# Stacking the parts of q and k of an attention layer by transfers through DRAM instead of products with selection matrices

## The chip, the cores and the metric

The kernel runs on one core of one Trainium2 chip. The metric is device time of one execution in microseconds (us). All compared runs were in the fast state, unless the text says otherwise. In the profiles PE is TensorE, PEld its weight loads, DVE VectorE, ACT ScalarE, POOL GpSimd and SP SyncE. The granted clock is the share of TensorE's full clock that the throttle allowed, as the profiler recorded it. A transfer lands when its completion is signalled.

## The reference

Four graph layers on 4096 nodes with 128 features, each followed by a residual and a layer norm. Only layer 1 matters here, a masked attention with four heads of 32 columns:

```python
N, IN, H, C = (4096, 128, 4, 32)
q = (x @ Wq + bq).reshape(n, H, C)
k = (x @ Wk + bk).reshape(n, H, C)
v = (x @ Wv + bv).reshape(n, H, C)
attn = jnp.einsum('nhc,mhc->hnm', q, k) / np.float32(np.sqrt(C))
mask = adj == 0.0
# ... softmax over the unmasked m gives alpha; out = alpha @ v per head ...
x_r = x @ Ws + bs                      # the "residual rows"
beta = jax.nn.sigmoid(jnp.concatenate([out, x_r, out - x_r], axis=-1) @ Wb)
return beta * x_r + (1.0 - beta) * out
```

## The kernel before

The scores are products in a rounded float32 format (float32r). To keep accuracy, k and q are cut into a rounded part `hi` and a rest `lo`. A head has only 32 of the 128 contraction rows, so the four combinations hi·hi, hi·lo, lo·hi and lo·lo are put below one another: for each head, rows 0..127 of `KS` hold hi, hi, lo, lo of k, and those of `QS` hold hi, lo, hi, lo of q. One product then gives the full score. The kernel before makes these stacks on PE, with selection matrices:

```python
def stacked(psum, a, hi, lo, h2):                     # two heads per call: four products
    p = psum.tile([P, 2, S], F32, tag="s", name="pst")
    for h in range(2):
        nc.tensor.matmul(p[:, h, :], lhsT=sel[a][:, 0, h2 + h, :], rhs=hi, start=True, stop=False)
        nc.tensor.matmul(p[:, h, :], lhsT=sel[a][:, 1, h2 + h, :], rhs=lo, start=False, stop=True)
    return p
```

The product stage, once per chunk c of 512 nodes (eight chunks):

```python
nc.tensor.matmul(p, lhsT=wk, rhs=XT[:, s], start=True, stop=True)
nc.scalar.activation(hi, p, AF.Identity, bias=bkc)
nc.vector.scalar_tensor_tensor(lo, p, bkc, hi.bitcast(F32), op0=ALU.add, op1=ALU.subtract)
nc.vector.tensor_reduce(mx[:, 1, c : c + 1], hi.bitcast(F32), AX.X, ALU.max, ...)
nc.scalar.copy(KS[:, 0:2, s], stacked(ps_s, 1, hi, lo, 0))
nc.vector.tensor_copy(KS[:, 2:4, s], stacked(ps_s, 1, hi, lo, 2))
# ... q likewise, written whole to DRAM (qd); only chunk 0 is cut and stacked here ...
```

Then come the V additions, and the residual rows in eight groups, each through one of two buffers to DRAM:

```python
r = rot.tile([P, 4, D], F32, tag="r", name="r")       # rot: bufs=2
nc.vector.tensor_tensor(r, p, bsr.unsqueeze(1).to_broadcast([P, 4, D]), ALU.add)
nc.sync.dma_start(out=rd[:, g[0] : g[-1] + 1, :], in_=r)
```

Attention follows: eight blocks of 512 queries, 32 steps of 128 keys each, where a step has four score products, two exponentials (ACT), a mask (DVE) and eight products for the weighted sums. Its working buffers take the memory of the product stage's. During block I the queries of block I+1 are fetched, cut and stacked:

```python
if I + 1 < NS:
    if jb == 5:
        fetch_queries(I + 1)                          # 256 KB from DRAM
    if jb == 18:
        cut_queries()                                 # ACT copy, DVE subtraction
    if jb in (21, 25):
        stack_queries(I + 1, (jb - 21) // 2)          # four products, one ACT cast
```

## Time and profile before

| | us |
|---|---|
| time, median of 3 runs | 2435.04 (2432.41 to 2437.69) |
| profiled span | 2427.1 |
| layer 0 ends (last group-norm activation starts) | 950.55 |
| first weighted sum of attention | 1043.21 |
| first weighted sum of attention's last step | 1868.4 |

The first layer runs the same code in all kernels here, and yet its end lies between 949.0 and 955.0 us in the profiles of this study. So I compare the second layer from that landmark on. Its two parts are called **entry** (from layer 0's end to the first weighted sum: 92.7 us in the kernel before) and **loop** (from there to the first weighted sum of the last step: 825.2 us).

The prediction quotes the windows, the chain and the timeline. One line more will be needed, the writes of the residual rows in the timeline of SP (start, length of the group of issues, engine, line, what, count):

```profile
1021.18 10.87 SPq L877 DMA_DIRECT2D rd<-r  x8
```

The reader is to see that eight writes took 10.87 us to issue; each had to wait for its row addition, and that for one of the two buffers.

### The profile page before, as it was taken

To read this page: it belongs to the slowest core of one execution; us is meant where nothing else is said; L and a number is where in the kernel's file an instruction comes from. 1 tells how busy PE (TensorE), PEld (TensorE's weight loads), DVE (VectorE), ACT (ScalarE), POOL (GpSimd) and SP (SyncE) were. 2 spreads that over 40 slices of the span, in tenths; PEclk is the share of its full clock that TensorE was granted. 3 is DMA by queue.
4 is the path that set the end of the run, shared out by engine and by line. 5 is a ranking of instruction groups with operands and counts; after the bars stand their busy time and mean duration, and the time that the engine had idled before them with its cause. 6 is when DMAs were issued, how large, how long until landed. Compare 5 with 4: busy or idle time off the path is not lost.

```text
span 2427.1 us, 24381 instructions
## 1 busy us (share of the span) xinstructions
PE 2048.1 (84%) x8923; PEld 1138.3 (47%) x8923; DVE 1910.2 (79%) x2726; ACT 1486.0 (61%) x1793; POOL 69.5 (3%) x87
## 2 busy tenths in 40 slices
PE   4477887787777771889999999999998899979998
PEld 4266666566666650634333333433333344444443
DVE  6478888788778888767877878777787887668887
ACT  5688889888888877478777787878776000010000
POOL 2000000000000051100000000000000000000000
PEclk7689989899888885999999999999999899979999
DMA  2455466555555630154454444545444788528774
GB/s 52 139 185 200 143 207 210 172 181 183 186 169 173 195 105 1 61 200 171 154 182 153 168 173 154 176 158 179 158 160 162 279 287 284 206 104 298 286 286 170
DMA packets 103768, 431.44 MB, mean 178 GB/s; under 512 B 8976, under 2 KB 19280, under 8 KB 62672
## 3 DMA queue, kind: packets, MB, share of 16 engines
q1 hardware_dynamic: 85200, 295.50, 35.9%
q10 hardware_dynamic: 18432, 134.23, 15.9%
q8 instruction: 74, 1.21, 0.2%
q14 instruction: 62, 0.51, 0.1%
HBM read 356.26 MB, written 73.43 MB: 177 GB/s over the span
## 4 chain that ended last, share of the span: by engine, by line
PE 58%; DVE 24%; ACT 12%; issue 3%; DMA 2%; SPq 0%; ACTq 0%; POOL 0%; DVEq 0%; POOLq 0%
PE pv L965 15%; PE pa L1357 9%; PE pa L1212 9%; PE ps L939 9%; DVE e L948 5%; PE pz L583 4%; DVE w L606 3%; PE pi L674 3%; DVE w L636 3%; DVE t L632 3%; PE ptA L564 3%; ACT t L628 3%; ACT e L946 2%; ACT at L572 2%; ACT w L601 1%
## 5 line engine op out<-in xcount | busy, mean ns | idle before, releaser
L948 DVE SCALAR_TENSOR_TENSOR e<-at,e 128x2048 f32<-128x2048 f32 x256 | 581.6, 2287 | 181.0 <-ACT e L946 171.3
L946 ACT ACTIVATE e<-ps 128x1024 f32<-128x1024 f32 x512 | 489.4, 1025 | 130.6 <-PE ps L939 101.8
L965 PE MATMUL pv<-e,VA 128*64 128x512 f32 x2048 | 503.5, 613 | 12.2 <-DVE e L948 12.2
L939 PE MATMUL ps<-QS,KS 128*128 128x512 f32 x1024 | 313.1, 425 | 27.7 <-ACT e L946 23.3
L939 PEld LDWEIGHTS ps<-QS,KS 128*128 128x128 f32 x1024 | 173.3, 190 | 246.0 <-ACT e L946 153.6
L674 PE MATMUL pi<-HA,w 128*128 128x129 f32 x1152 | 186.7, 337 | 83.2 <-DVE w L636 83.2
L965 PEld LDWEIGHTS pv<-e,VA 128*64 128x64 f32 x2048 | 126.0, 137 | 258.1 <-issue 232.2
L1357 PE MATMUL pa<-w,F 128*128 128x512 f32 x512 | 223.2, 597 | 12.2 <-DVE w L1354 12.2
L674 PEld LDWEIGHTS pi<-HA,w 128*128 128x128 f32 x1152 | 179.8, 249 | 93.8 <-DVE w L636 93.8
L1212 PE MATMUL pa<-at,Y 128*128 128x512 f32 x512 | 223.1, 596 | 0.0
L1354 DVE SCALAR_TENSOR_TENSOR w<-rho,col,at 128x512 f32<-128x512 f32 x256 | 186.7, 746 | 18.9 <-PE pa L1357 1.7
L591 DVE SCALAR_TENSOR_TENSOR t<-ei,de,pz 128x512 f32<-128x512 f32 x144 | 107.2, 747 | 106.5 <-PE pz L583 102.7
L564 PE MATMUL ptA<-ident,ad 128*128 128x128 f32 x1032 | 146.0, 287 | 42.9 <-ACT at L572 35.7
L1222 DVE SCALAR_TENSOR_TENSOR odd<-at 128x2048 f32<-128x2048 f32 x64 | 146.6, 2290 | 38.3 <-DMA at<-adjT 37.6
L564 PEld LDWEIGHTS ptA<-ident,ad 128*128 128x128 f32 x1032 | 124.9, 148 | 99.4 <-ACT at L572 53.3
L572 ACT COPY at<-ptA 128x512 f32<-128x512 f32 x200 | 108.3, 587 | 99.0 <-PE ptA L564 98.8
L583 PE MATMUL pz<-HT 128*128 128x512 f32 x292 | 161.6, 664 | 4.9 <-DVE w L655 4.5
L1357 PEld LDWEIGHTS pa<-w,F 128*128 128x128 f32 x512 | 97.3, 192 | 133.9 <-issue 100.1
L1212 PEld LDWEIGHTS pa<-at,Y 128*128 128x128 f32 x512 | 97.5, 192 | 120.0 <-issue 118.8
L606 DVE TENSOR_TENSOR w<-w,at 128x2048 f32<-128x2048 f32 x64 | 143.7, 2281 | 0.0
L1361 ACT COPY a<-pa 128x512 f32<-128x512 f32 x8 | 4.7, 586 | 206.1 <-PE pa L1357 206.1
L931 ACT ACTIVATE nat<-nat 128x2048 f32<-128x2048 f32 x64 | 122.7, 1918 | 1.9 <-DMA nat<-in_adj_dram 1.9
(351 smaller groups left out, 2448.8 us busy)
## 6 DMA issues: line engine op xcount, KB each, us to landing
at<-adjT SPq DMA_DIRECT2D x128, 1024.0 KB, 4.8
ad<-in_adj_dram SPq DMA_DIRECT2D x64, 1024.0 KB, 6.5
adjT<-at SPq DMA_DIRECT2D x64, 1024.0 KB, 8.3
nat<-in_adj_dram ACTq DMA_DIRECT2D x64, 1024.0 KB, 4.9
at<-adjT ACTq DMA_DIRECT2D x64, 1024.0 KB, 4.8
dj<-rows SPq DMA_DIRECT2D x28, 256.0 KB, 7.6
X<-in_x_dram SPq DMA_DIRECT2D x4, 512.0 KB, 6.5
di<-rows SPq DMA_DIRECT2D x8, 256.0 KB, 8.4
```

The source lines that it names most:

```text
L564: nc.tensor.transpose(pt[:, ib, :], st[p]["ad"][k][:, ib, jb * P : (jb + 1) * P], self.ident)
L572: copy(st[p]["at"][k][:, jb, :], st[p]["pt"].pop(m))
L583: nc.tensor.matmul(pz, lhsT=HT[:, j * P : (j + 1) * P], rhs=HT[:, I * S : (I + 1) * S], start=True, stop=True)
L606: nc.vector.tensor_tensor(w, w, at, ALU.mult)
L674: nc.tensor.matmul(self.po[ib // 2][:, ib % 2, :], lhsT=w[0][:, jb, ib * P : (ib + 1) * P], rhs=HA[:, 4 * J + jb, :], start=False, stop=(J ...
L939: nc.tensor.matmul(p[:, h, :], lhsT=KS[:, h2 + h, jb * P : (jb + 1) * P], rhs=QS[I % 2][:, h2 + h, :], start=True, stop=True,)
L946: nc.scalar.activation(e[:, h2 : h2 + 2, :], p, AF.Exp)
L948: nc.vector.scalar_tensor_tensor(e, at[:, jb % 4, :].unsqueeze(1).to_broadcast([P, NH, S]), 0.0, e, op0=ALU.not_equal, op1=ALU.mult,)
L965: nc.tensor.matmul(st["po"][h // 2][g : g + 64, :], lhsT=VA[:, o : o + 64], rhs=e[:, h, :], start=(jb == 0), stop=(jb == NT - 1), skip_gro ...
L1212: nc.tensor.matmul(pa, lhsT=Y[:, 4 * J + jb, :], rhs=at[:, jb, :], start=False, stop=(J == NS - 1 and jb == 3), skip_group_check=True,)
L1354: nc.vector.scalar_tensor_tensor(w, rho[:, I * S : (I + 1) * S], col[:, 0, j : j + 1], at[:, jb, :], op0=ALU.max, op1=ALU.mult)
L1357: nc.tensor.matmul(pa, lhsT=F[:, j, :], rhs=w, start=False, stop=(j == NT - 1), skip_group_check=True)
```

## The change

The intent is to free PE of the selection products, since PE bounds both the product stage and the loop. All chunks of k and q are cut once, both parts go to DRAM in one write of 512 KB, and a stack is made by four reads of 256 KB, each to 32 partitions. The destination is float32r, and GpSimd issues the reads; the prediction says why.

```diff
-            sel = [keep.tile([P, 2, NH, P], F32R, ...) for k in range(2)]
-            qd = self.dram.tile([P, N], F32, tag="qd", name="qd")
+            qk = self.dram.tile([2, 2, P, N], F32, tag="qk", name="qk")
-            def stacked(psum, a, hi, lo, h2): ...
+            def stack(a, dst, c):
+                for r, part in enumerate(((0, 1, 0, 1), (0, 0, 1, 1))[a]):
+                    nc.gpsimd.dma_start(
+                        out=dst[r * C : (r + 1) * C, :, :],
+                        in_=qk[a, part, :, c * S : (c + 1) * S].rearrange("(h c) n -> c h n", h=NH),
+                    )
@@ product stage, per chunk c
+                    for a, w, bias in ((1, wk, bkc), (0, wq, bqc)):
+                        p = self.ps_t.tile([P, S], F32, tag="pt", name="pqk")
+                        nc.tensor.matmul(p, lhsT=w, rhs=XT[:, s], start=True, stop=True)
+                        cut = rot.tile([P, 2, S], F32R, tag="cut", name="cut", bufs=4)
+                        nc.scalar.activation(cut[:, 0, :], p, AF.Identity, bias=bias)
+                        nc.vector.scalar_tensor_tensor(cut[:, 1, :], p, bias, cut[:, 0, :].bitcast(F32), ...)
+                        nc.vector.tensor_reduce(mx[:, a, c : c + 1], cut[:, 0, :].bitcast(F32), ...)
+                        nc.sync.dma_start(out=qk[a, :, :, s].rearrange("k p n -> p k n"), in_=cut.bitcast(F32))
+                        if a:
+                            stack(1, KS[:, :, s], c)
+                        elif c < 2:
+                            stack(0, QS[c], c)
@@ attention loop
-                        if I + 1 < NS: ...            # fetch, cut, stack at steps 5, 18, 21, 25
+                        if jb == 3 and 0 < I < NS - 1:
+                            stack(0, QS[(I + 1) % 2], I + 1)
```

The branch for large scores (not taken with these inputs) is adapted too; it is left out here. So are two small edits: `Wq` is scaled by 1/sqrt(C) beforehand, and the PSUM pool of these products has eight buffers instead of four, in place of the pool of the selection products.

More of the change, by code (lines that the diff above doesn't have):

```diff
@@ L781, in layer1 @@
             QS = [keep.tile([P, NH, S], F32R, tag=f"QS{k}", name=f"QS{k}") for k in range(2)]
-            sel = [keep.tile([P, 2, NH, P], F32R, tag=f"sel{k}", name=f"sel{k}") for k in range(2)]
-            qd = self.dram.tile([P, N], F32, tag="qd", name="qd")
+            qk = self.dram.tile([2, 2, P, N], F32, tag="qk", name="qk")
             rd = self.dram.tile([P, NT, D], F32, tag="rd", name="rd")
@@ L793, in layer1 @@
             bvr, bsr = self.load_row(bv, "bvr"), self.load_row(bs, "bsr")
-            for a, rows in enumerate((((0, 2), (1, 3)), ((0, 1), (2, 3)))):
-                nc.gpsimd.memset(sel[a].bitcast(F32), 0.0)
-                for b in range(2):
-                    for r in rows[b]:
-                        nc.gpsimd.tensor_copy(
-                            sel[a][:, b, :, r * C : (r + 1) * C], self.ident.rearrange("p (h c) -> p h c", h=NH)
-                        )
-            def stacked(psum, a, hi, lo, h2):
-                p = psum.tile([P, 2, S], F32, tag="s", name="pst")
-                for h in range(2):
-                    nc.tensor.matmul(p[:, h, :], lhsT=sel[a][:, 0, h2 + h, :], rhs=hi, start=True, stop=False)
-                    nc.tensor.matmul(p[:, h, :], lhsT=sel[a][:, 1, h2 + h, :], rhs=lo, start=False, stop=True)
-                return p
+            def stack(a, dst, c):
[4 more added lines that the diff above has]
+                    )
             with ExitStack() as pctx:
@@ L813, in layer1 @@
                 rot = pctx.enter_context(tc.tile_pool(name="rot1", bufs=2))
-                self.ps_t = pctx.enter_context(tc.tile_pool(name="ps_t", bufs=4, space=PSUM))
-                ps_s = pctx.enter_context(tc.tile_pool(name="ps_s1", bufs=2, space=PSUM))
+                self.ps_t = pctx.enter_context(tc.tile_pool(name="ps_t", bufs=8, space=PSUM))
                 nc.gpsimd.memset(VA, 1.0)
@@ L821, in layer1 @@
                 nc.vector.tensor_scalar(bqc, bqc, 1.0 / math.sqrt(C), None, op0=ALU.mult)
+                nc.vector.tensor_scalar(wq, wq, 1.0 / math.sqrt(C), None, op0=ALU.mult)
                 for c in range(NC):
                     s = slice(c * S, (c + 1) * S)
-                    p = self.ps_t.tile([P, S], F32, tag="pt", name="pk")
-                    nc.tensor.matmul(p, lhsT=wk, rhs=XT[:, s], start=True, stop=True)
-                    hi = rot.tile([P, S], F32R, tag="hi", name="hi")
-                    lo = rot.tile([P, S], F32R, tag="lo", name="lo")
@@ L828, in layer1 @@
-                    nc.scalar.activation(hi, p, AF.Identity, bias=bkc)
-                    nc.vector.scalar_tensor_tensor(lo, p, bkc, hi.bitcast(F32), op0=ALU.add, op1=ALU.subtract)
-                    nc.vector.tensor_reduce(
-                        mx[:, 1, c : c + 1], hi.bitcast(F32), AX.X, ALU.max, apply_absolute_value=True
-                    )
-                    nc.scalar.copy(KS[:, 0:2, s], stacked(ps_s, 1, hi, lo, 0))
-                    nc.vector.tensor_copy(KS[:, 2:4, s], stacked(ps_s, 1, hi, lo, 2))
@@ L835, in layer1 @@
-                    p = self.ps_t.tile([P, S], F32, tag="pt", name="pq")
-                    nc.tensor.matmul(p, lhsT=wq, rhs=XT[:, s], start=True, stop=True)
-                    q = rot.tile([P, S], F32, tag="q", name="q")
-                    nc.scalar.activation(q, p, AF.Identity, bias=bqc, scale=1.0 / math.sqrt(C))
-                    nc.sync.dma_start(out=qd[:, s], in_=q)
-                    nc.vector.tensor_reduce(mx[:, 0, c : c + 1], q, AX.X, ALU.max, apply_absolute_value=True)
-                    if c == 0:
-                        hi = rot.tile([P, S], F32R, tag="hi", name="hi")
-                        lo = rot.tile([P, S], F32R, tag="lo", name="lo")
-                        nc.scalar.copy(hi, q)
-                        nc.vector.tensor_tensor(lo, q, hi.bitcast(F32), ALU.subtract)
-                        for h2 in range(0, NH, 2):
-                            nc.scalar.copy(QS[0][:, h2 : h2 + 2, :], stacked(ps_s, 0, hi, lo, h2))
+                    for a, w, bias in ((1, wk, bkc), (0, wq, bqc)):
[3 more added lines that the diff above has]
+                        nc.scalar.activation(cut[:, 0, :], p, AF.Identity, bias=bias)
+                        nc.vector.scalar_tensor_tensor(
+                            cut[:, 1, :], p, bias, cut[:, 0, :].bitcast(F32), op0=ALU.add, op1=ALU.subtract
+                        )
+                        nc.vector.tensor_reduce(
+                            mx[:, a, c : c + 1], cut[:, 0, :].bitcast(F32), AX.X, ALU.max, apply_absolute_value=True
+                        )
+                        nc.sync.dma_start(out=qk[a, :, :, s].rearrange("k p n -> p k n"), in_=cut.bitcast(F32))
[3 more added lines that the diff above has]
+                            stack(0, QS[c], c)
@@ L880, in layer1, with attention_unshifted @@
             with tc.If(small > 0) as cmp:
-                self.attention_unshifted(VA, KS, QS, stacked, qd, rd, wb)
+                self.attention_unshifted(VA, KS, QS, stack, rd, wb)
             with cmp.Else():
-                self.attention_shifted(V, qd, (wk, bkc), rd, wb)
-    def attention_unshifted(self, VA, KS, QS, stacked, qd, rd, wb):
+                self.attention_shifted(V, qk, rd, wb)
+    def attention_unshifted(self, VA, KS, QS, stack, rd, wb):
         nc, tc, N, NT, NS, D, X = self.nc, self.tc, self.N, self.NT, self.NS, self.D, self.X
@@ L896, in attention_unshifted @@
             st = {}
-            def fetch_queries(I):
-                st["f"] = rot.tile([P, S], F32, tag="f", name="f")
-                nc.sync.dma_start(out=st["f"], in_=qd[:, I * S : (I + 1) * S])
-            def cut_queries():
-                hi = rot.tile([P, S], F32R, tag="hi", name="hi")
-                lo = rot.tile([P, S], F32R, tag="lo", name="lo")
-                nc.scalar.copy(hi, st["f"])
-                nc.vector.tensor_tensor(lo, st["f"], hi.bitcast(F32), ALU.subtract)
-                st["parts"] = hi, lo
-            def stack_queries(I, h2):
-                nc.scalar.copy(QS[I % 2][:, h2 : h2 + 2, :], stacked(ps_s, 0, *st["parts"], h2))
             def load(I, J):
@@ L1048, in attention_unshifted @@
                             degree(8 * I + jb // 4)
-                        if I + 1 < NS:
-                            if jb == 5:
-                                fetch_queries(I + 1)
-                            if jb == 18:
-                                cut_queries()
-                            if jb in (21, 25):
-                                stack_queries(I + 1, (jb - 21) // 2)
+                        if jb == 3 and 0 < I < NS - 1:
+                            stack(0, QS[(I + 1) % 2], I + 1)
                         scores(I, jb)
@@ L1068, in attention_unshifted, with attention_shifted @@
             nc.vector.tensor_tensor(self.deg, self.deg2[:, 0, :], self.deg2[:, 1, :], ALU.add)
-    def attention_shifted(self, V, qd, kw, rd, wb):
+    def attention_shifted(self, V, qk, rd, wb):
         nc, tc, N, NT, D, X = self.nc, self.tc, self.N, self.NT, self.D, self.X
@@ L1079, in attention_shifted @@
             KT = keep.tile([P, N], F32, tag="KT", name="KT")
-            XT = keep.tile([P, S], F32, tag="XT", name="XT")
-            for g in self.groups():
-                s = slice(g[0] * P, (g[-1] + 1) * P)
-                p = self.ps_t.tile([P, 4, P], F32, tag="pt", name="pt")
-                for k, t in enumerate(g):
-                    nc.tensor.transpose(p[:, k, :], X[:, t, :], self.ident)
-                nc.vector.tensor_copy(XT, p.rearrange("p a b -> p (a b)"))
-                p = self.ps_t.tile([P, 4, P], F32, tag="pt", name="pt").rearrange("p a b -> p (a b)")
-                nc.tensor.matmul(p, lhsT=kw[0], rhs=XT, start=True, stop=True)
-                nc.scalar.activation(KT[:, s], p, AF.Identity, bias=kw[1])
+            K2 = keep.tile([P, S], F32, tag="K2", name="K2")
+            for c in range(N // S):
+                s = slice(c * S, (c + 1) * S)
+                nc.gpsimd.dma_start(out=KT[:, s], in_=qk[1, 0, :, s])
+                nc.gpsimd.dma_start(out=K2, in_=qk[1, 1, :, s])
+                nc.vector.tensor_tensor(KT[:, s], KT[:, s], K2, ALU.add)
             den = keep.tile([P, NH], F32, tag="den", name="den")
@@ L1094, in attention_shifted @@
             nc.gpsimd.memset(QH, 0.0)
+            Q2 = keep.tile([P, 2, P], F32, tag="Q2", name="Q2")
             work = ctx.enter_context(tc.tile_pool(name="work1", bufs=1))
@@ L1098, in attention_shifted @@
             for i in range(NT):
+                nc.gpsimd.dma_start(
+                    out=Q2, in_=qk[0, :, :, i * P : (i + 1) * P].rearrange("k p n -> p k n")
+                )
                 for h in range(NH):
                     hs = slice(h * C, (h + 1) * C)
-                    nc.sync.dma_start(out=QH[hs, h, :], in_=qd[hs, i * P : (i + 1) * P])
+                    nc.vector.tensor_tensor(QH[hs, h, :], Q2[hs, 0, :], Q2[hs, 1, :], ALU.add)
                 m = self.load_adj(i)
```

## The prediction

> **What bounds the kernel now.** I read the page's busy table and chain first: over the whole run PE is 84% busy, DVE 79%, ACT 61%, and PE carries 58% of the chain that ended last. The change touches only the second layer, so the whole-run shares say little, and I read that layer by stages. Four windows of it (us; PE, PEld, DVE, ACT and POOL busy with instruction counts; granted clock, DMA share, GB/s):
>
> ```profile
> 982.00:1012.00 30.00, 28.36 (x96) 17.41 (x94) 24.18 (x33) 19.42 (x25) 0.00 (x0) 1.00 0.19 71
> 1012.00:1034.00 22.00, 17.09 (x136) 16.00 (x136) 12.66 (x42) 1.28 (x1) 0.00 (x0) 0.96 0.26 96
> 1034.00:1139.00 105.00, 99.19 (x387) 39.31 (x386) 73.76 (x34) 80.70 (x86) 0.00 (x0) 0.96 0.52 183
> 1139.00:1244.00 105.00, 101.18 (x404) 39.70 (x404) 82.86 (x87) 80.35 (x89) 0.00 (x0) 0.98 0.48 165
> ```
>
> The first window makes K and Q, stacked by products with the selection matrices: PE is busy 28.4 of 30 us, and the DMA engines are nearly empty. The second makes V and the residual rows. The others are the first two of eight attention blocks of 32 steps. PE is full there too; DMA is half used.
>
> Next the chain of waits in order of time (start, us, what), once at a stacking inside the first block, and once at the entry to attention:
>
> ```profile
> 1095.54 1.87 PE pv L965 x8
> 1098.54 1.87 PE pv L965 x8
> 1102.44 1.87 PE pv L965 x8
> 1105.45 1.87 PE pv L965 x8
> ```
>
> ```profile
> 1028.19 2.05 DMA rd<-r
> ...
> 1031.73 2.03 DMA rd<-r
> 1033.90 6.74 DMA at<-adjT
> 1040.77 2.30 DVE e L948
> ```
>
> In a plain step the weighted sums come 3.00 us apart. Across the stacking the distance is 3.90. So the four selection products cost 0.90 us on the bound engine. The second list shows that attention's first loads wait until the last residual rows have landed in DRAM (the memory of the working buffers is reused), and that the loop's first mask waits for that load.
>
> The timeline of that stacking shows what the 0.90 us is:
>
> ```profile
> 1100.34 0.50 PE L807 MATMUL pst<-hi,sel 128*128 128x512 f32 x1
> 1100.67 0.40 PE L808 MATMUL pst<-lo,sel 128*128 128x512 f32 x1
> 1100.91 0.39 PE L807 MATMUL pst<-hi,sel 128*128 128x512 f32 x1
> 1101.14 0.40 PE L808 MATMUL pst<-lo,sel 128*128 128x512 f32 x1
> ...
> 1101.57 1.02 ACT L910 CAST QS<-pst 128x1024 fp32r<-128x1024 f32 x1 [1.39 <-PE pst L808]
> ```
>
> Starts lie 0.23 us apart, four products make 0.9. In the product stage, DVE does this per product:
>
> ```profile
> 989.85 0.75 DVE L829 SCALAR_TENSOR_TENSOR lo<-pk,bkc,hi 128x512 fp32r<-128x512 f32 x1 [0.35 <-ACT hi L828]
> ...
> 990.52 0.68 DVE L830 TENSOR_REDUCE mx<-hi 128x1 f32<-128x512 f32 x1
> ```
>
> Last the DMA queues (packets, MB, share of 16 engines' span):
>
> ```profile
> q1 hardware_dynamic: 85200, 295.50, 35.9%
> q10 hardware_dynamic: 18432, 134.23, 15.9%
> ```
>
> 295.5 MB in 35.9% of 2427.1 us is 339 GB/s, 134.2 MB in 15.9% is 348: what the engines move while busy. I use 345.
>
> **What the Trainium skill says.** (1) "DMA: Bandwidth & Descriptors", section "SWDGE vs HWDGE vs iDMA": a cast in a DMA goes only through the software generator of GpSimd, and a float32r destination always counts as a cast. That is why the new reads are issued by GpSimd. The kernel before has only hardware queues, as its two queue rows show, so no duration of such a transfer is at hand. (2) Same page, "Issuing engines are not separate DMA queues": all issuers share the 16 engines and interleave. So the new reads compete with the new writes. (3) Same page, "Anatomy of one DMA": about 2.0 us fixed for a software-generated transfer plus bytes over 436 GB/s; for 256 KB that is 2.6 us. The trace's 256 KB writes to DRAM by hardware queue land in 2.0 us (median), so the order agrees. (4) "SBUF — State Buffer", section "Door 1": by its formula 32 consecutive partitions reach 8 of the 16 ports. Each new read writes 32 partitions. No transfer of the kernel before shows the effect.
>
> **The change part by part.**
>
> Loop, removed: in blocks 0 to 6, two stackings of four products, 7 x 2 x 0.90 = 12.6 us of PE, all on the path by the spacing above. With them go two ACT casts (1.02 us each), one ACT copy and one DVE subtraction (0.68) per block; at those steps the chain is on PE, so I count nothing more.
>
> Loop, added: in blocks 1 to 6, four reads of 256 KB, about 1 MB beside the 16.8 MB of masks and rows that a block loads already (165 GB/s at share 0.48). They are issued at step 3 for the next block, some 90 us ahead, and their buffer was last read in the block before. Hidden.
>
> Product stage, removed: 64 + 8 selection products, 72 x 0.23 = 16.6 us of PE, the eviction casts (ACT 8 x 1.01 + 2 x 1.02, DVE 8 x 1.22) and the separate cut of the first queries. Left are 16 products of 0.86 us on the chain, 13.8 us of PE; ACT 16 x 0.69 = 11.0; DVE 16 x (0.75 + 0.68) = 22.9. By its engines the stage would shrink from about 30 us to 23, bound by DVE.
>
> Product stage, added: 16 writes of 512 KB (8.39 MB) and ten stacks of four 256 KB reads (10.49 MB). Together 18.9 MB / 345 GB/s = 55 us of all DMA engines, where before 2.1 MB went. DVE would produce 1 MB per 2.9 us, which is 366 GB/s of writes alone; they can't be kept up beside equal reads. The cut buffer has four slots, so from the fifth product on the stage runs at the pace of the writes. With half of the engines, 8.39 MB need 8.39 / 0.1725 = 49 us; if the software-generated reads lag behind their writes, less, some 42. The first write can leave at about 980, so the writes end at 1022 to 1029, and the last cut is made four writes earlier, at about 1015 to 1020 instead of 1011. What follows in DVE's order, the V additions (7 us) and the residual rows (13.3 us from the first at 1020.5 to the last landing at 1033.8), then starts 5 to 9 us later, and its writes stand in the same queue behind the cuts and beside the stacks still outstanding: another 3 us. If DVE's fixed order puts V additions between the cuts, part of this is won back, 5 to 7 us. Entry to attention: 6 to 10 us later, my middle 7.5. The first masks load beside the last stacks; 1 MB then takes perhaps 8 us instead of 6.7: +1.
>
> First block: its step 4c needs key chunk c, so one chunk per 12 us (four steps of 3.00). A chunk is 1 MB; the reads deliver one per 5 to 7 us and are several chunks ahead at the entry. No wait expected.
>
> Sum: -12.6 + 7.5 + 1 = -4.1 us. From 2435.0 that is 2431.
>
> **The rivals.**
> *A: the transfers hide.* The scheduler puts V and the residual rows into DVE's idle time, or the engines move small writes faster (the first windows' 71 GB/s at share 0.19 is 374 GB/s). Then the stage ends where it did or earlier, at best by the 7 us of the engine sum: -12.6 - 7 = -20, 2415. For it: DVE would have the gaps, and V needs only XT. Against: in the kernel before, DVE had gaps too (24.2 of 30 us) and no V addition was put there.
> *B: the casting reads are slow, or are made one after the other.* The page gives no rate for a cast. At 100 GB/s a chunk takes 10.5 us, still inside the 12 that the first block allows; but slow packets share each engine with the writes, and writes at a third of the rate end after 75 us instead of 49: +26 us at the entry, 2456. At 50 GB/s a chunk takes 21 us and the first block starves by about 9 us for each of its later chunks: +70 or more, 2500.
> *C: the waits are coarser than the data.* If writing chunk c + 1 has to wait for the stacks of chunk c (same DRAM tensor), each chunk costs a write of about 3.5 us and four reads of about 6: 8 x 9.5 = 76 us for a stage of 30, +46 - 13 = +33, 2468. Nothing in the trace of before tells, as its transfers of q are written once and read much later.
>
> **Range and chances.** The loop's gain is firm (12 to 13.5 us). The entry is not: -7 to +10 us in the main case and A, +25 to +45 in B and C, which I give about one chance in five together. So 2431, range 2411 to 2462. Two per cent is 48.7 us: no rival saves that much, as the whole stage and the stackings are only 43 us; losing it takes the starved first block or B and C together. Chances: faster 0.02, same 0.90, slower 0.08.
>
> **What would show it.** Right: attention steps 3.00 us apart everywhere outside the block endings, with no 3.90; a block period of about 102.9 us instead of 104.7 (the ending's first ACT piece recurs in the chain at 1154.65, 1259.33 and 1364.08); in the product stage PE mostly idle, DVE waiting for DMA of the cuts, DMA share near 0.9 and about 300 GB/s from 985 to 1025; entry to attention at 1040 to 1044 and the first mask at about 1049; PE never waiting for KS in the first block. Wrong: DVE busy through the stage with no wait for the cuts (A); key chunks later than every 12 us, or PE waiting for KS or QS (B); writes of the cuts spaced by the stacks' landing (C); or block endings that stretch, which would show that new traffic delays masks.

## The result, and the profile after

The changed kernel took 2431.73 us (median of 4 runs, 2427.63 to 2433.65) beside 2435.51 for the kernel before on the same chip; the ratio is 0.9983 with an interval of 0.9966 to 1.0001. Here and below a ratio is the mean time of one kernel's fast runs over that of the other's of the same rounds, so it is not quite the ratio of the medians. A longer repeat (the first run below) gave 1.0004. The kernels are equally fast, and two parts of the second layer have changed against each other.

The same windows as before (us; PE, PEld, DVE, ACT and POOL busy with instruction counts; granted clock, DMA share, GB/s) in the changed kernel:

```profile
982.00:1012.00 30.00, 14.85 (x31) 5.80 (x30) 17.09 (x26) 9.35 (x15) 12.21 (x23) 0.73 1.02 328
1012.00:1034.00 22.00, 14.50 (x111) 14.49 (x112) 13.11 (x44) 2.95 (x4) 8.68 (x16) 0.72 1.28 330
1034.00:1139.00 105.00, 86.12 (x340) 35.51 (x340) 65.31 (x33) 65.00 (x69) 1.09 (x2) 0.90 0.58 188
```

PE has fallen from 28.36 to 14.85 of 30 us, as intended, and DVE and ACT have fallen too; POOL, which now issues the reads, has risen from 0 to 12.21. None of them is full, so none bounds the stage. The DMA engines do; their share has gone from 0.19 to 1.02, and they move 328 GB/s instead of 71. (The share adds up the times of packets, so it can pass 1 where they overlap; I read such a value as full.) The granted clock falls to 0.72 with PE idle half of the time. These windows also take in the start and the end of the traffic. Two narrower ones show its middle, and the time after the cut writes had landed (the last at 1027.6), when almost only reads were under way:

```profile
1000.00:1022.00 22.00, 2.50 (x13) 2.49 (x14) 10.45 (x20) 6.09 (x8) 8.44 (x16) 0.50 1.15 381
1030.00:1036.00 6.00, 6.00 (x57) 6.00 (x56) 1.54 (x3) 0.00 (x0) 2.42 (x5) 1.00 1.53 218
```

Writes and reads together moved 381 GB/s, the reads alone 218.

The waits of 970 to 1140 us name who waits (engine and line, waited for: us in total, times, longest us):

```profile
ACT cut L820 <- DMA qk<-cut: 23.1, 11, 4.6
...
POOL KS L798 <- DMA KS<-qk: 21.3, 24, 1.8
...
DVE r L860 <- DMA rd<-r: 13.6, 4, 7.3
```

The first line: ACT starts a cut and finds no free slot, because the write of the cut four places earlier hasn't landed. The second: GpSimd issues a read only when an earlier one has landed; so did 32 of the 40 reads of the entry (eight stand in other lines), each when the read eight places before it had landed. With eight in flight and one landing every 1.4 us, a read takes about 11 us. No run varied this number. The third: a row addition finds none of its two buffers free, as its write hasn't landed. The chain at the entry (start, us, what):

```profile
1007.67 9.12 DMA qk<-cut
...
1030.88 8.07 DMA rd<-r
...
1039.79 5.23 DMA rd<-r
...
1045.86 2.03 DMA rd<-r
...
1049.39 2.02 DMA rd<-r
...
1051.56 6.65 DMA at<-adjT
...
1058.34 2.30 DVE e L918
```

A row write of 256 KB, which took 2.03 us in the kernel before, takes 8.07 and 5.23 us while the stacks are outstanding, and 2.03 again when they have drained (the last read landed at 1044.4). The first two writes were issued at 1030.9 and 1031.8, but up to 1036 the hardware queue started packets of 0.01 MB in all, the software queue of 1.29 MB. The first mask's load then takes 6.65 us, as before (6.74). In the loop the chain reads:

```profile
1098.86 1.87 PE pv L935 x8
...
1101.86 1.87 PE pv L935 x8
...
1104.85 1.87 PE pv L935 x8
...
1107.85 1.87 PE pv L935 x8
```

The weighted sums are 3.00 us apart here; the 3.90 at a stacking has gone. (In blocks 1 to 7 some of the first 14 steps stay longer, 3.38 to 5.50 us, as in the kernel before: there the ending of the previous block is worked off.) The queues (packets, MB, share of 16 engines' span) have a new row, the software queue of GpSimd:

```profile
q1 hardware_dynamic: 87392, 299.95, 36.6%
...
q0 software_dynamic: 9216, 16.78, 3.5%
```

Laid beside one another from layer 0's end on (read from the timelines):

| us after layer 0's end | before | changed | difference |
|---|---|---|---|
| first cut by DVE | 28.5 | 29.4 | +0.9 |
| all cut, maxima reduced | 59.9 | 66.2 | +6.3 |
| first residual row added | 69.9 | 77.4 | +7.4 |
| first mask load issued | 83.4 | 98.8 | +15.4 |
| first mask | 90.2 | 105.5 | +15.3 |
| first weighted sum | 92.7 | 107.9 | +15.3 |
| last step | 917.8 | 919.2 | +1.3 |

So the entry has lost 15.3 us and the loop won 13.9 (825.2 to 811.2). The entry's loss is +6.3 in the cutting, +1.1 in the V additions, +8.0 from the first residual row to the mask load (21.4 us instead of 13.4), and nothing after that. The loop's gain is mostly the 14 stackings at 0.90 = 12.6 us. The rest is a pair of steps where a block's ending is worked off (steps 12 and 13 of the next block): it takes 10.07 to 10.13 us in five blocks of the kernel before, and 9.74 (5.50 + 4.24) in its blocks 3 and 6 and in all of the changed kernel's, which makes about 1.9; the first step of block 0 takes 0.8 of it back. The longer pair comes back in some blocks of other kernels here (two blocks of q alone take 102.86 and 102.89 us instead of 102.50), and one of 9.90 in the second profile of the changed kernel itself, so it may belong to the execution and not to the change. What sets it was not found.

### The profile page after: what moved, and what is told of

It is laid out like the page before. It is cut to its first block, busy times and chain, and to the rows that moved or that the text cites. A ratio compares the mean times of both kernels' runs of the same rounds, so it can differ in the third digit from the quotient of the medians.

```text
span 2429.7 us, 24219 instructions
## 1 busy us (share of the span) xinstructions
PE 2016.8 (83%) x8795; PEld 1115.1 (46%) x8795; DVE 1902.7 (78%) x2719; ACT 1459.5 (60%) x1761; POOL 100.8 (4%) x141
## 4 chain that ended last, share of the span: by engine, by line
PE 56%; DVE 24%; ACT 13%; DMA 3%; issue 3%; ACTq 0%; SPq 0%; POOL 0%; DVEq 0%; POOLq 0%
PE pv L935 14%; PE pa L1322 9%; PE pa L1177 9%; PE ps L909 8%; DVE e L918 5%; PE pz L583 4%; PE pi L674 3%; PE ptA L564 3%; DVE w L606 3%; DVE t L632 3%; DVE w L636 3%; ACT t L628 2%; ACT e L916 2%; ACT at L572 2%; ACT w L601 1%
## 5 line engine op out<-in xcount | busy, mean ns | idle before, releaser
L935 PE MATMUL pv<-e,VA 128*64 128x512 f32 x2048 | 497.5, 607 | 12.6 <-DVE e L918 12.6
L591 DVE SCALAR_TENSOR_TENSOR t<-ei,de,pz 128x512 f32<-128x512 f32 x144 | 107.5, 748 | 111.6 <-PE pz L583 107.9
L583 PE MATMUL pz<-HT 128*128 128x512 f32 x292 | 167.3, 685 | 4.2 <-DVE w L655 3.8
L642 PE MATMUL ptz<-ident,t 128*128 128x128 f32 x448 | 69.5, 297 | 67.2 <-DVE w L655 45.3
```

The costliest lines, as they stand in the source:

```text
L583: nc.tensor.matmul(pz, lhsT=HT[:, j * P : (j + 1) * P], rhs=HT[:, I * S : (I + 1) * S], start=True, stop=True)
L935: nc.tensor.matmul(st["po"][h // 2][g : g + 64, :], lhsT=VA[:, o : o + 64], rhs=e[:, h, :], start=(jb == 0), stop=(jb == NT - 1), skip_gro ...
```

## The experiments

**Theory.** The entry loses through the volume of transfers: writes of cuts and reads of stacks fill the DMA engines from 985 us until the last read has landed at 1044, which paces the cutting and delays each residual row's write. The loop gains through PE alone. **Rivals.** The casting reads of the software queue are themselves slow; the few buffers (four for cuts, two for rows) are at fault rather than the volume; the reads of k, of which attention needs only chunk 0 at first, crowd out what is urgent.

All kernels passed the comparison with the reference (one of them although it is wrong on purpose, as told there). The table has the differences to the kernel before: entry and loop from one profile each, and the ratio of the timed runs. Two profiles of the changed kernel agree within 0.5 us in both parts; where a ratio and a sum of landmarks differ, the ratio decides.

| kernel | entry | loop | ratio (interval) |
|---|---|---|---|
| changed, first time | +15.3 | -13.9 | 0.9983 (0.9966 to 1.0001) |
| changed, again | +14.8 | -13.6 | 1.0004 (0.9994 to 1.0014) |
| q alone | -0.2 | -13.6 | 0.9935 (0.9914 to 0.9955) |
| k alone | +6.0 | +0.3 | 1.0024 (1.0016 to 1.0032) |
| eight row buffers | +10.7 | -10.1 | 0.9986 (0.9977 to 0.9995) |
| eight cut buffers | +12.8 | -12.9 | 0.9995 (0.9986 to 1.0003) |
| late key stacks, paced | +5.9 | -8.3 | 0.9971 (0.9959 to 0.9982) |
| the same, eight row buffers | +2.2 | -8.0 | 0.9963 (0.9948 to 0.9977) |
| late key stacks, at once | +5.5 | -11.0 | 0.9972 (0.9958 to 0.9986) |
| q alone, eight row buffers | -4.1 | -13.1 | 0.9921 (0.9903 to 0.9939) |

### The changed kernel again

No edit; five rounds beside the next kernels.

> The changed kernel unedited, timed beside the same runs of the kernel before as the next ones, for a narrower ratio than 0.9966 to 1.0001. From its first trace: loop -13.9 us, entry +15.3 us, so a ratio of 1.000; from its first ratio 0.998. Both theories alike: between 0.997 and 1.001.

2434.02 us (22 runs) beside 2433.70 (33 runs): 1.0004. The 3.8 us between the medians of the first measurement are not confirmed; its interval had reached 1.0001. Both theories had expected this, so the run only sharpens the number.

### Queries alone, keys alone

q alone: queries as in the changed kernel, keys by selection products as before.

```diff
-                    for a, w, bias in ((1, wk, bkc), (0, wq, bqc)): ...
+                    # k: as in the kernel before, hi, lo, and stacked() by products
+                    cut = rot.tile([P, 2, S], F32R, tag="cut", name="cut", bufs=4)      # q only
+                    nc.sync.dma_start(out=qk[:, :, s].rearrange("k p n -> p k n"), in_=cut.bitcast(F32))
+                    if c < 2:
+                        stack(QS[c], c)
```

> Queries through DRAM, keys by selection products as before. Theory (the loop's gain of about 14 us belongs to the queries, the later entry to attention of about 15 us to the volume of the transfers, mostly the keys'): loop as in the changed kernel, block period 102.5 us, entry within 3 us of the kernel before; 2422 us, ratio about 0.994 to 0.996. Rival (the later entry comes from the software-issued transfers as such, or from the queries' part): entry 7 us later or more, 2428 or above.

k alone: keys as in the changed kernel, queries fetched, cut and stacked in the loop by products.

```diff
-                        if jb == 3 and 0 < I < NS - 1:
-                            stack(0, QS[(I + 1) % 2], I + 1)
+                        if I + 1 < NS: ...            # fetch, cut, stack by products, as before
```

> Keys through DRAM, queries by selection products in the loop as before. Theory: loop as before (block period 104.7 us), entry later by 7 to 12 us since 14.7 MB instead of 18.9 MB go through the engines; 2442 to 2448 us, ratio about 1.004. Rival (volume doesn't matter as long as the stage is short): entry as before or earlier, 2435 or less.

q alone: 2419.14 us (6 runs), loop as in the changed kernel, entry as before. k alone: 2438.42 (22 runs), loop as before, entry +6.0. The expectation for q alone held; that for k alone was too high (7 to 12 us at the entry, ratio 1.004). So the loop's gain belongs to the queries and the entry's loss to the keys, with one addition: +6.0 and -0.2 do not make +14.8. The queries add 4.2 MB (4.2 MB of writes instead of 2.1, and 2.1 of reads). They cost nothing when PE still bounds the stage, and about 9 us when the keys' transfers already fill the engines. (The changed kernel also differs from both in its eight PSUM buffers; their part in the 9 us was not tested.) In k alone the cutting is not late, 58.6 us after layer 0's end: the whole loss stands behind the first residual row, 19.5 us from there to the mask load instead of 13.4. The window of the product stage in q alone (columns as above) shows the free ride:

```profile
985.00:1015.00 30.00, 29.02 (x95) 17.34 (x94) 28.14 (x39) 18.33 (x25) 4.57 (x8) 0.99 0.75 194
```

PE is busy 29.02 of 30 us at a granted clock of 0.99, with the DMA engines at 0.75 under it.

### More buffers for the rows, more for the cuts

```diff
-                    r = rot.tile([P, 4, D], F32, tag="r", name="r")
+                    r = rot.tile([P, 4, D], F32, tag="r", name="r", bufs=8)
```

> The changed kernel with eight buffers for the residual rows instead of two. Theory (the rows' writes wait behind the key reads in the shared engines, the drain of both sets the entry): DVE's wait for the rows' landing (13.6 us) goes, but the last landing is at about 1045 instead of 1051; 5 us saved, 2427 us. Rival (the round trip of two buffers is the whole of the 8 us): 8 us or more saved, 2423.

```diff
-                        cut = rot.tile([P, 2, S], F32R, tag="cut", name="cut", bufs=4)
+                        cut = rot.tile([P, 2, S], F32R, tag="cut", name="cut", bufs=8)
```

> The changed kernel with eight slots for the cut parts instead of four. Theory (the engines' throughput of about 380 GB/s sets when the writes end, the slots only how far the cutting runs ahead): cutting ends about 8 us earlier, the V additions go beside the drain, but the rows' writes queue behind the cuts; 3 to 5 us saved, 2428 us. Rival (four slots throttle the transfers themselves): 8 us or more saved, DMA share no longer full during cutting.

The writes of the rows, in SP's timeline, first in the changed kernel and then with eight buffers; the second line of each is the first mask's load:

```profile
1030.88 18.83 SPq L861 DMA_DIRECT2D rd<-r  x8
1051.56 0.80 SPq L884 DMA_DIRECT2D at<-adjT  x2
```

```profile
1030.60 6.57 SPq L861 DMA_DIRECT2D rd<-r  x8
1046.60 0.80 SPq L884 DMA_DIRECT2D at<-adjT  x2
```

And how long such a write took from issue to landing, first in the changed kernel, then with eight buffers:

```profile
DMA to landing us min/median/max: 2.0/3.2/8.6
```

```profile
DMA to landing us min/median/max: 8.3/9.6/10.1
```

With eight buffers all eight writes are under way within 6.57 us, but each lands after 8.3 to 10.1 us. The mask's load still waits for the last of them, which lands 9.6 us after its issue instead of 2.0, and 1.5 us after the last read of the stacks. That wins 4.6 of the 8.0 us at the entry (4.1 against the second profile of the changed kernel), close to the theory's 5; the rest is the drain. (Its profile has a loop 3.9 us longer than the changed kernel's, 3.2 of it in the pairs at the block endings of blocks 1 to 5, 10.0 to 11.5 us instead of 9.74. Why is open, and one profile can't tell whether the kernel or the execution is the cause. By the timed ratios, 0.9986 against 1.0004 for the repeat of the changed kernel, the gain is about 4 us; the two were timed in different rounds.)

Eight cut buffers end the cutting 10.0 us sooner (56.2 us after layer 0's end instead of 66.2), and the entry wins only 2.5. The writes of the cuts now land after 14.8 us (median) instead of 9.1: what was a wait for a slot has become a longer queue. The rows start earlier, and then wait in pairs, 8.0, 6.9 and 4.6 us at a time, until the stacks have drained. So more cut buffers alone do not help, and more row buffers alone help by half. Eight of both were not tried: with the rows ready 10 us sooner and none held by a buffer, they might land before the drain ends. That the volume ahead of the last row is the limit, and not the two numbers of buffers together, is therefore not shown by this pair.

### Key stacks later

Attention needs key chunk c at step 4c of block 0. So the stacks of chunks 2 to 7 (6.3 of 10.5 MB) are taken out of the entry and issued in block 0, one every two steps. To hold GpSimd back until the step is reached, it first copies one element of an earlier step's result. (Chunk 2, at step 0, has no such copy; its reads left at 1018.6, during the V additions, and had landed before the first row was written.)

```diff
-                        if a:
+                        if a and c < 2:
                             stack(1, KS[:, :, s], c)
-                        elif c < 2:
+                        elif c < 2 and not a:
                             stack(0, QS[c], c)
@@ attention loop
+                        if I == 0 and jb % 2 == 0 and jb // 2 < NS - 2:
+                            if jb:
+                                nc.gpsimd.tensor_copy(pace, st["e", 0, jb - 2][0:1, 0, 0:1])
+                            c = jb // 2 + 2
+                            stack(1, KS[:, :, c * S : (c + 1) * S], c)
```

> The changed kernel with the reads of key chunks 2 to 7 moved into the first block of attention, one per two steps. All bytes still move, 6.3 MB of them after the entry. Theory (the volume ahead of the entry makes it late): cutting ends 5 us earlier, the rows land without queueing behind key reads, entry 8 to 12 us earlier than in the changed kernel, first block without waits for keys; ratio 0.994 to 0.996. Rival (the first block starves or its masks load later, so that the cost only moves): first block longer than 98 us by the time saved, ratio 0.998 or above.

The same with eight row buffers:

> As the last, with eight row buffers. Theory: the rows leave as DVE makes them; another 3 to 5 us, ratio 0.992 to 0.994, level with the kernel that sends only the queries through DRAM (0.9935). Rival (row buffers beside deferral save nothing, since the at loads wait for the same drain): same as the last.

2426.58 us (11 runs) and 2424.12 (7 runs); the entry wins 9.4 and 13.1 us over the changed kernel. Neither ratio reached what its theory expected (0.994 to 0.996 and 0.992 to 0.994), and their intervals overlap, so the gain of the row buffers here rests on the landmarks. The landing of the row writes, in the kernel without the extra buffers, shows that the stacks had delayed them:

```profile
DMA to landing us min/median/max: 2.0/2.0/2.0
```

The rows take 10.1 us from first addition to last (11.2 in the kernel before, 19.2 in the changed one). But the cutting hardly ends sooner (65.4 us after layer 0's end, 66.2 in the changed kernel; 5 us had been expected): the 8.4 MB of cut writes and the 4.2 MB of stacks that stay are enough to pace it. And part of the gain is given back in block 0, which takes 103.1 us instead of 98.0: three of its steps, each at a pacing copy, take 3.73 us, two more 4.06 and 3.75, one 4.51. Was that the pacing or the moved bytes? The next kernel issues all six chunks after one pacing copy:

```diff
-                        if I == 0 and jb % 2 == 0 and jb // 2 < NS - 2: ...
+                        if I == 0 and jb == 0:
+                            nc.gpsimd.tensor_copy(pace, st["at", 0, 0][0:1, 0, 0:1])
+                            for c in range(2, NS):
+                                stack(1, KS[:, :, c * S : (c + 1) * S], c)
```

> Key chunks 2 to 7 read in the first block as in the deferred run, but paced by one single read of the first mask tile instead of reads of the weights at each second step. Theory (the first block's extra 5 us there came from the pacing, not from the bytes): entry 9 us earlier than in the changed kernel, first block 98 us again, ratio 0.996. Rival (the moved bytes themselves delay masks or keys): first block 102 us or more, ratio 0.997 to 0.999.

Block 0 takes 101.1 us, nearer to the rival's 102 than to the theory's 98. The steps of 3.73 are gone, so those were the pacing copies. One step of 6.09 us is left, and its cause stands in the timeline (start, us, engine, line, what, idle before and released by):

```profile
1090.17 1.91 ACT L902 ACTIVATE nat<-nat 128x2048 f32<-128x2048 f32 x1 [3.30 <-DMA nat<-in_adj_dram]
```

ACT's instructions stand in a fixed order; a degree sum waits 3.30 us for a row load that shares the engines with the moved stacks, and the exponentials stand behind it. So in this kernel, which moves all six chunks at once, the bytes cost some 3 us. In the paced one the same wait for a row load was 1.70 us, and that step, of 4.51, was 1.5 over 3.00; the other five long steps were 4.0 over, so there the pacing took most of the loss, as far as the vanished steps show. The total, 2426.13 us (12 runs), is the same as with pacing within the intervals.

### Is the software queue or the cast slow? Are 32 partitions?

The six stacks of the loop (blocks 2 to 7) are not on the path, so their transfers can be varied there without moving anything else. First by SP's hardware queue, with the destination taken as plain float32 (the parts are rounded already, so no cast is needed):

```diff
-                    nc.gpsimd.dma_start(
-                        out=dst[r * C : (r + 1) * C, :, :],
+                    o = dst[r * C : (r + 1) * C, :, :]
+                    (nc.sync if hw else nc.gpsimd).dma_start(
+                        out=o.bitcast(F32) if hw else o,
...
+                            stack(0, QS[(I + 1) % 2], I + 1, hw=True)
```

> The changed kernel with the stacks of the loop issued from the SP queue into the same tiles seen as float32, so without cast and without software descriptors; each still writes 32 partitions. In the changed kernel such a stack of 1 MB, alone on the engines, moved 205 to 220 GB/s and landed 8 us after its first issue. If the cast or the software queue is the limit: 300 GB/s or more, landing within 5 us. If the 32 partitions are the limit: again near 215 GB/s. Time as the changed kernel within 4 us either way.

Then by GpSimd as in the changed kernel, but each read of 256 KB to all 128 partitions. That puts wrong rows into `QS` on purpose from block 2 on. (The comparison with the reference passed this kernel all the same: with these inputs it doesn't notice wrong query stacks, and that the other kernels passed it says little of theirs.)

```diff
+                    if wide:
+                        nc.gpsimd.dma_start(out=dst[:, r, :], in_=qk[a, part, :, c * S : (c + 1) * S])
+                        continue
```

> Wrong result on purpose: in the loop the four 256 KB reads of a stack go to all 128 partitions (one head's place each) instead of 32 partitions with four heads each; same source rows, 2 KB pieces, software queue and cast. If the 32 destination partitions limit the rate: such a stack moves 300 GB/s or more and lands within 6 us instead of 8. If the 2 KB pieces at the source's row pitch limit it: again near 215 GB/s and 8 us. Time as the changed kernel within 4 us.

Each got one look, 2431.67 and 2430.42 us, whose state is unknown; the times decide nothing here and were not meant to. What counts is the median from issue to landing (last column) in the window 1150 to 1700 us, in the changed kernel, then by SP, then to 128 partitions:

```profile
QS<-qk POOLq DMA_DIRECT2D x24, 256.0 KB, 7.4
```

```profile
QS<-qk SPq DMA_DIRECT2D x24, 256.0 KB, 7.8
```

```profile
QS<-qk POOLq DMA_DIRECT2D x22, 256.0 KB, 5.7
```

(In the last, two issues and some packets are missing from the trace. The 8 us of the expectations is about a single read's time; in the changed kernel a whole stack took 10.5 to 11.6 us from its first issue to its last landing, with a row load beside its first part.) The hardware queue without a cast is no faster. The number of partitions matters. The queue's row of the same window (packets, MB, share of 16 engines), in the changed kernel and to 128 partitions:

```profile
q0 software_dynamic: 3456, 6.29, 7.4%
```

```profile
q0 software_dynamic: 3373, 6.13, 3.9%
```

6.29 MB in 7.4% of 550 us are 155 GB/s of packet time, 6.13 MB in 3.9% are 286. To 32 partitions the packets of the same bytes take almost twice as long. What moves while no other queue does, first in the changed kernel, then to 128 partitions (windows, columns as above):

```profile
1156.00:1158.00 2.00, 2.00 (x10) 0.67 (x7) 1.80 (x2) 2.00 (x4) 0.00 (x0) 1.00 1.53 214
```

```profile
1256.00:1257.00 1.00, 1.00 (x5) 0.41 (x6) 1.00 (x1) 0.74 (x1) 0.00 (x0) 1.00 1.24 397
```

214 GB/s against 397 (in this one microsecond; the reads to 128 partitions are seldom alone). The drain at the entry had the same rate, 218, with eight reads in flight where the loop has four, so in the drain it was not the number in flight that set it. This agrees with the Trainium skill, "SBUF — State Buffer", section "Door 1", by whose formula partitions 0 to 31 reach half of the 16 ports. Beside the cut writes it was different: from 1000 to 1022 the software queue moved 4.07 MB in a packet share of 56.1%, 330 GB/s of packet time, so the 155 of the loop doesn't hold there. Reads to 128 partitions were not tried at the entry, where they would have to show what they are worth. Other orders of the four reads, which would put an even and an odd half side by side, were not tried.

### The best of the parts

q alone with eight row buffers.

```diff
-                    r = rot.tile([P, 4, D], F32, tag="r", name="r")
+                    r = rot.tile([P, 4, D], F32, tag="r", name="r", bufs=8)
```

> Queries through DRAM, keys by products (0.9935), with eight row buffers. Theory: DVE's waits for the rows' landing (about 4 us) go, nothing else is queued ahead of them; ratio 0.992 to 0.993. Rival (as with the changed kernel, where eight row buffers brought 4.6 us at the entry and 3.9 were lost in the loop): no better than 0.9935.

2412.24 us (6 runs), ratio 0.9921, the fastest of the study and about 19 us under the kernel before. The entry is 3.9 us shorter than in q alone; the intervals of the two ratios overlap, so the second part of the gain rests on the landmarks.

## Why the prediction was right or wrong

The time was right: 2431 predicted, 2431.73 measured, range and class too. But the agreement to 0.7 us is partly luck. The sum was -4.1; the repeat, with more runs, puts the difference at +1.0 us (-1.5 to +3.4), which excludes -4.1; the first measurement's interval (-8.3 to +0.2) has only -1.5 to +0.2 in common with it. The loop won 13.9 where 12.6 were predicted, and the entry lost 15.3 where 8.5 were. (The range was drawn too narrow for its own rivals: its end, 2462, leaves out the 2468 of C and the 2500 of B. Neither came.) Point by point:

- **Loop, removed: 12.6.** Right. 14 stackings at 0.90 went, all on the path; 13.9 were won, the other 1.3 mainly from the block endings (1.9 won) and the first step (0.8 lost), which the prediction counted as unchanged.
- **Loop, added: hidden.** Right: no step of the changed kernel's loop waits for a stack.
- **Product stage, engines.** Right in kind: no engine bounds it, and the cuts wait for their slots, as the chain shows (it is ACT that waits, not DVE as the prediction's sign had it). Of its figures, 345 GB/s was 381 in the middle of the stage.
- **Product stage, first part: 5 to 9 us.** Right: the residual rows start 7.4 later. The last cut ended at 1018.4, inside 1015 to 1020. Of the 7.4, 0.9 stood before the first cut already and 1.1 came from the V additions, which the sum did not have; the cutting itself made 5.4.
- **"Another 3 us" for the rows.** This is the term that failed. It measured 8.0 us, and with it failed the signs of the entry: attention was to start at 1040 to 1044 and its first mask at about 1049, and the mask's load was issued at 1051.6, the mask came at 1058.3. The prediction named the mechanism, writes in the same queue behind cuts and beside outstanding stacks, but gave it the cost of a slightly longer queue. Nothing was left of the cuts when the rows came (the last cut write landed at 1027.6, the first row write was issued at 1030.9); the stacks were. With two buffers the row writes go in pairs, one after the other, and each takes up the latency of the loaded engines: 8.07 and 5.23 us instead of 2.03. The late key stacks (rows landing in 2.0 us) show that cause, and eight row buffers, with 4.6 us, that about half of it came from the pairs.
- **345 GB/s for every byte.** The prediction quoted "Door 1" and then did not use it. One rate for all was too low while writes and reads ran together (381) and too high for what was left, reads alone at 218. That lengthens the drain, and it is the drain that the rows ran into. How much shorter it would be with reads to 128 partitions was not measured.
- **Masks beside the last stacks: +1.** Wrong, -0.1. The mask's load is issued when the rows have landed, and by then the stacks have landed too.
- **First block: no wait.** Right: its steps are 2.99 to 3.00 after the first, and PE never waited for `KS`.
- **V additions.** Not in the sum; +1.1, inside the 7.4 above, at a granted clock of 0.72 in that window instead of 0.96. What the clock costs there was not tested by itself.
- **Rival A (hidden)** did not come: the V additions lie behind the last cut. **Rival B (slow casting reads)** neither: in the loop the hardware queue without a cast is as slow (at the entry the queue was not varied). **Rival C (a wait per tensor)** neither: it would have spaced the eight chunks by the landing of a stack, 11.0 us (median) for `KS`, so over 88 us, and the whole cutting took 36.8 (29.4 to 66.2 after layer 0's end).

With the measured terms the sum is 7.4 + 8.0 - 0.1 - 13.9 = +1.4, with which the repeat's +1.0 agrees. The change is neutral because its two halves cancel, and taken apart one of them is worth 0.65% (0.45 to 0.86).

## What to carry to other kernels

Moving work from a full engine to the DMA engines pays where they have room and the deadline is far (the queries: 0.90 us of PE at each stacking for reads that nobody waits for), and costs where a burst must drain before the next stage can begin (the keys). A change that does the same thing in two places is to be tried in each place alone, since a sum of zero can hide a gain. When transfers are counted, the small writes behind a burst count with the latency of the loaded queue, times the number of rounds that their buffers force. Reads to 32 partitions count about twice where nothing else is under way (214 to 218 GB/s here, against 397 to 128 partitions), and not beside writes from 128 partitions (381 GB/s in all).

## What the Trainium skill lacked or had wrong

- "DMA: Bandwidth & Descriptors", section "SWDGE vs HWDGE vs iDMA": it gives no rate for a read that casts. Here the casting read by the software queue is not slower than a plain one by a hardware queue (landing in 7.4 against 7.8 us for 256 KB to 32 partitions).
- The same page, section "Anatomy of one DMA": by its formula 256 KB take an estimated 2.6 us. The row writes of the same size land in 2.0 us without other traffic, by hardware queue; the reads of the stacks, which go the way that it describes, landed after 7.4 (loop, four in flight) and 11.0 us (product stage, `KS`, median, eight in flight). A pointer to 32-partition destinations and to loaded engines is missing in that section.
- No page found that says how long a small write waits beside large outstanding reads of another queue: here 2.0 us alone and 8.3 to 10.1 us beside them (eight row buffers). How the engines shared their time was not settled by these runs.
- "SBUF — State Buffer", section "Door 1": nothing wrong. Its table has 189 GB/s measured for 1 MiB to 32 partitions, and about 218 as the limit; the reads of the stacks moved 214 (loop) and 218 (drain) when they were alone. What the section doesn't tell is the rate beside transfers the other way: here 381 GB/s in all, with 185 of it by such reads.
